# Four binary-convolution layers and attention on one core: the last image's softmax denominators by pixel halves in two PSUM tiles

## The chip, the cores and the metric

The kernel runs on one NeuronCore of a Trainium2 chip. A core has five engines with a queue of instructions each: TensorE (matmuls, PE in the profile; its weight loads are PEld), VectorE (DVE), ScalarE (ACT), GpSimd (POOL) and SyncE (SP), which issues DMAs. Every engine can also wait on semaphores and issue DMAs or branch; such instructions are run by its sequencer, and the profile marks them with a q (ACTq, SPq). The metric is the device time of one execution in microseconds (us). The median of three runs before the change is 949.11 us (948.44 to 949.25).

## The reference, cut to what matters

Input is x of shape 16 x 256 x 28 x 28. Three layers of binary convolutions come first (signs of activations, 3x3 convolutions, batch norms, gates); the change does not touch them. The fourth layer is attention within each image, over its N = 784 pixels:

```python
q = jnp.einsum('rc,bcn->bnr', Wq, xf)          # 64 channels
k = jnp.einsum('rc,bcn->brn', Wk, xf)
v = jnp.einsum('rc,bcn->bnr', Wv, xf)
attn = jnp.einsum('bnr,brm->bnm', q, k) * scale
attn = jax.nn.softmax(attn, axis=-1)
out = jnp.einsum('bnm,bmr->brn', attn, v)
out = jnp.einsum('cr,brn->bcn', Wp, out)
return out.reshape(B, C, H, W) + x
```

A softmax usually subtracts each row's maximum. The kernel's usual path leaves that out and keeps a watch: if a sum of exps (a denominator) or its reciprocal is too large, or an earlier stage has doubts about its arithmetic, a flag on the chip sends the program into a second, careful computation of the whole thing. With these inputs the flag says that all is well, and the careful program is jumped over.

## The kernel before, in words

`conv_seq_kernel` calls `forward(careful=False)`, which ends by loading the flag into a register of every engine (`values_load`, L1366), and then branches (`tc.If`, L80): in the usual case over the careful program, whose code lies between. After the branch, engines wait for the outstanding DMAs and drain.

Attention is `attend_unshifted` (from L1408). The order of instructions on every engine is written out by hand (`manual_schedule`): each engine runs its own instructions in the order of the code. An image has 7 chunks (`NC_`) of 112 keys. For chunk c of image b:

- `scores(b, c)`: two matmuls, one for each half (392) of the queries' pixels, into a tile of two PSUM banks (pool `pssc`, two buffers, "sc"), then one Exp on ScalarE over 128 x 784 into `es[b, c]` (L1502).
- `values(b, c)`: two matmuls side by side, each on 64 of the array's columns, that add the exps times v into one bank, `avs[b]` (pool `psav`). Rows 0 to 63 hold the first pixel half, rows 64 to 127 the second, so a tile of 128 x 392 (`HN`) holds an image.
- `denominators(b)`: the same with `ones` for v, into one bank "sm" (pool `pssm`, one buffer). For this, exps are added up first: `sum_up` adds chunks 0 to 3 on GpSimd (the sum called `sums[b, False]`, L1510 and L1512) and 4 to 6 on VectorE (`sums[b, True]`); `sum_all` (L1515) adds the two. That is for images up to 13. For images 14 and 15 (`b >= B - 2`, L1540) chunk 6 and the two sums stay apart, and TensorE adds them up, in three pairs of matmuls in place of one.
- `take_values(b)` copies `avs[b]` to SBUF (`o`) on ScalarE; `invert(b)` takes the reciprocals `r` on VectorE (L1545); `normalize(b)` multiplies o by r (L1549); `watch(b)` sums denominators and reciprocals on ScalarE with its accumulator into columns of `worst` (L1554).
- `project(b, mo)`: two matmuls with Wp for each half mo of the 256 output channels (L1579, pool `psmi`, one buffer "mi", or `pssc`); the function that it returns adds the residual on VectorE (L1590, or L1588 for banks apart). `store(b)` writes the image out (L1611).

Images overlap: while image b's scores are made, image b - 1 is normalized and b - 2 projected. After the loop, L1695 to L1720 hold what is left of images 13 and 14 beside image 15's scores; `doubts_so_far` (L1597) folds the earlier stages' doubts into `sure`. Then comes a block of its own (L1722), with a hint to each engine on where the branch will go. In it: the last values; reciprocals in two parts of 196 pixels of each half (`parts`); a copy of `avs` to SBUF (L1735); the watch on the denominators, in one accumulated sum, and on the reciprocals, half by ScalarE and half by VectorE (L1734 to L1737); the normalization in two parts; four projections of a part and a channel half each, and their additions. `raise_flag` (L1603) stands among these: VectorE adds up `worst` and compares it to LIMIT (L1605, L1606), a matmul counts the partitions that are well (L1607), and VectorE writes the flag (L1608). Channel half 0 is stored after its last addition, half 1 after the very last, both from ScalarE's queue.

Of the kernel before, what the change touches and what calls it, by code (L numbers as in the profile page):

```python
# [39 lines left out]
P = 128  # L40
B = 16
# [23 lines left out]

LIMIT = 1e18


VECS = (
    ["g0", "b0", "a_move", "a_alpha1", "a_alpha2"]  # L70
# [5 lines left out]


def conv_seq_kernel(tc: tile.TileContext, d: dict, out: bass.AP):
    again = forward(tc, d, out, False)
    with tc.If(again < 1, preferred_fallthrough_block=False, label="again") as usual:  # L80
        pass
    with usual.Else():
        forward(tc, d, out, True)


@with_exitstack
def forward(ctx: ExitStack, tc: tile.TileContext, d: dict, out: bass.AP, careful: bool):
# [1269 lines left out]
        return None  # L1357


    worst = const.tile([P, 4 * B], F32, name="worst")  # L1360
    nc.gpsimd.memset(worst, 0.0)
    flag = const.tile([P, 1], I32, name="flag")
    finish = (sg3, bg3, pt, x2d, x2, load_x2, idle)
    keys = [wpool.tile([P, NC_, 4, 32], F32, tag=t, name=f"keys{t}") for t in ("wa", "wa2")]
    attend_unshifted(tc, d, out, wqk, wv, wp, keys, worst, (doubts, nonzero), flag, pv, finish)
    return nc.values_load(flag[0:1, 0:1], min_val=0, max_val=P)  # L1366


@with_exitstack
# [39 lines left out]
def attend_unshifted(ctx, tc, d, out, wqk, wv, wp, keys, worst, doubts, flag, pv, finish):  # L1409
# [34 lines left out]
    def one_bank(pool, tag):  # L1444
        return pool.tile([P, 512], F32, tag=tag, name=tag)
# [71 lines left out]
    def side_by_side(ps, w, e, start, stop):  # L1517
        for h in range(2):
            T.matmul(ps[64 * h:64 * h + 64, :HN], lhsT=w, rhs=e[:, h, :], start=start, stop=stop)  # L1519
# [11 lines left out]
    def take_values(b, n=slice(0, HN)):  # L1531
        if n.start == 0:
            os[b] = (buf("o", 2, shape=(P, HN)), buf("r", 2, shape=(P, HN)))
        A.copy(os[b][0][:, n], avs[b][:, n])

    def denominators(b):

        dns[b] = last[:, 0, :HN] if b == B - 1 else one_bank(pssm, "sm")

        parts = [sums[b, False], sums[b, True], es[b, NC_ - 1]] if b >= B - 2 else [sums[b, True]]  # L1540
        for i, e in enumerate(parts):
            side_by_side(dns[b], ones.rearrange("p a i -> p (a i)"), e, i == 0, i == len(parts) - 1)

    def invert(b, n=slice(0, HN)):
        V.reciprocal(os[b][1][:, n], dns[b][:, n])  # L1545
# [46 lines left out]
        return add  # L1592


    w1, ok, sure, some = (ph.tile([P, 1], F32, name=n) for n in ("w1", "ok", "sure", "some"))

    def doubts_so_far():  # L1597
        V.tensor_reduce(sure, doubts[0], AX.X, ALU.max)
        V.tensor_scalar(sure, sure, 1.0, None, ALU.is_le)
        V.tensor_reduce(some, doubts[1], AX.X, ALU.min)  # L1600
        V.scalar_tensor_tensor(sure, some, K9 / 3.0, sure, ALU.is_ge, ALU.mult)

    def raise_flag(ps):  # L1603

        V.tensor_reduce(w1, worst, AX.X, ALU.add)  # L1605
        V.scalar_tensor_tensor(ok, w1, LIMIT, sure, ALU.is_le, ALU.mult)  # L1606
        T.matmul(ps[0:1, 0:1], lhsT=ok, rhs=turned[:, 0, 0:1], start=True, stop=True)  # L1607
        return lambda: V.tensor_scalar(flag[0:1, :], ps[0:1, 0:1], -1.0, float(P), ALU.mult, ALU.add)  # L1608

    def store(b, mo=slice(0, 2), queue=nc.sync):  # L1610
        queue.dma_start(out=out[b][:, mo], in_=x[b][:, mo])  # L1611
# [4 lines left out]
    with tc.manual_schedule(engines={ET.PE, ET.Activation, ET.DVE, ET.Pool, ET.SP}):  # L1616

        ps = [two_banks(psmi, "mi"), two_banks(pssc, "sc")]
        cuts = [slice(h * HN, h * HN + HN) for h in range(2)]
        for n in cuts:  # L1620
            v = x[0][:, 1, n]
            V.scalar_tensor_tensor(v, v, sg3[:, 1:2], x2[0][:, 1, n], ALU.mult, ALU.add)
        for h, n in enumerate(cuts):
            finish_a(0, n, (0,))
            v, w = (x[0][:, k, n] for k in range(2))
            A.activation(w, w, AF.Identity, bias=bg3[:, 1:2])
            V.tensor_tensor(v, v, x2[0][:, 0, n], ALU.add)
            for k, y in enumerate((v, w)):
                V.scalar_tensor_tensor(y, y, alpha[:, k:k + 1], y, ALU.mult, ALU.max)
            queries_keys(0, h, ps[h])  # L1630
        A.activation(ph.tile([P, 2], F32, name="e"), sg3, AF.Exp, scale=0.0)
        keep_busy(8)
        for h in range(2):
            keys_to(0, 1, h, ps[h])
            queries(0, h, ps[h])
            keys_to(0, 0, h, ps[h])
        finish_a(1)
        scores(0, 0)
        project_v(0)
        finish_b(1, ks=(0,))  # L1640
        turn_v(0)
        finish_b(1, ks=(1,))
        V.transpose(ones.rearrange("p a i -> p (a i)"), turned.rearrange("p a i -> p (a i)"))
        for b in range(B - 1):
            scores(b, 1)
            if b > 0:
                take_values(b - 1)
            if b == 0:
                finish_a(2)
            if b > 1:  # L1650
                project(b - 2, 0)()
            sum_up(b, 1)
            scores(b, 2)
            if b > 0:
                sum_up(b - 1, 6)
            scores(b, 3)
            sum_up(b, 2, 3)
            ps = two_banks(psmi, "mi")
            for h in range(2):
                queries_keys(b + 1, h, ps)  # L1660
            for h in range(2):
                keys_to(b + 1, 1, h, ps)
            for h in range(2):
                queries(b + 1, h, ps)
            for h in range(2):
                keys_to(b + 1, 0, h, ps)
            project_v(b + 1)
            if b > 0:
                sum_all(b - 1)
            turn_v(b + 1)  # L1670
            scores(b, 4)
            scores(b, 5)
            sum_up(b, 5)
            if b + 2 < B:
                finish_b(b + 2)
            if b + 3 < B:
                finish_a(b + 3)
            for c in range(4):
                values(b, c)
            if b > 0:  # L1680
                denominators(b - 1)
                invert(b - 1)
                normalize(b - 1)
            scores(b, 6)
            scores(b + 1, 0)
            if b > 1:
                project(b - 2, 1)()
                store(b - 2)
            if b > 0:
                watch(b - 1)  # L1690
            for c in range(4, NC_):
                values(b, c)


        b = B - 1  # L1695
        scores(b, 1)
        take_values(b - 1)
        project(b - 2, 0)()
        sum_up(b, 1)
        scores(b, 2)  # L1700
        denominators(b - 1)
        invert(b - 1)
        scores(b, 3)
        sum_up(b, 2, 3)
        normalize(b - 1)
        scores(b, 4)
        scores(b, 5)
        sum_up(b, 5)
        scores(b, 6)
        project(b - 2, 1)()  # L1710
        store(b - 2)
        doubts_so_far()
        for mo in range(2):
            project(b - 1, mo, pool=pssc)()
        store(b - 1)
        watch(b - 1)
        for c in range(3):
            values(b, c)
        last = two_banks(pssc, "sc")
        denominators(b)  # L1720

    with tc.block(), tc.manual_schedule(engines={ET.PE, ET.Activation, ET.DVE, ET.Pool, ET.SP}):  # L1722
        tc.mark_branch_hint_location("again", "LikelyTaken", engines=[ET.PE, ET.Activation, ET.DVE, ET.Pool, ET.SP])
        for c in range(3, NC_):
            values(b, c)

        parts = [slice(0, HN // 2), slice(HN // 2, HN)]
        os[b] = (buf("o", 2, shape=(P, HN)), buf("r", 2, shape=(P, HN)))
        r = os[b][1]
        watched = [worst[:, i:i + 1] for i in range(4 * b, 4 * b + 4)]  # L1730
        junk = buf("junk", 1, shape=(P, HN))
        for n in parts:
            invert(b, n)
        V.tensor_reduce(watched[2], r[:, parts[1]], AX.X, ALU.add)  # L1734
        A.copy(os[b][0], avs[b][:, :HN])  # L1735
        A.activation(junk, dns[b], AF.Copy, accum_out=watched[0])
        A.activation(junk[:, parts[0]], r[:, parts[0]], AF.Copy, accum_out=watched[1])  # L1737
        for n in parts:
            normalize(b, n)

        adds = [
            project(b, mo, ps, n) for n, mo, ps in (
                (parts[0], 0, two_banks(psmi, "mi")),
                (parts[0], 1, two_banks(pssc, "sc")),
                (parts[1], 0, [one_bank(pssm, "sm"), one_bank(psav, "av")]),
            )
        ]
        adds[0]()
        up = raise_flag(last[:, 1, :])
        adds.append(project(b, 1, two_banks(psmi, "mi"), parts[1]))  # L1750
        adds[2]()
        store(b, slice(0, 1), nc.scalar)
        up()
        for add in adds[1::2]:
            add()
        store(b, slice(1, 2), nc.scalar)


@with_exitstack
# [175 lines left out]
```

## Time and profile before

| what | value |
|---|---|
| median of three runs | 949.11 us (948.44 to 949.25) |
| the profiled execution's own time | 949.33 us |
| its span, first to last instruction | 947.5 us |
| granted TensorE clock, mean | 0.999 |
| TensorE, VectorE, ScalarE, GpSimd busy | 930.7, 757.1, 675.1, 139.0 us |
| image 14's denominators end, reciprocal, normalization | 924.16; 924.19 to 926.8; 926.90 to 928.34 us |
| image 15's denominators, last values | 932.20 to 934.17; to 936.83 us |
| last addition ends | 940.86 us |
| flag written | 939.9 us |
| last store issued; landed | 940.89; about 945.7 us |

Times within the execution are counted in us from the start of the span. A row of a timeline gives start, length, engine, line, operation, output <- inputs with their shapes (partitions x elements), and in brackets how long the engine had been idle before and what ended that. One row of TensorE can hold several matmuls ("x4"); a float32 matmul appears twice, so two matmuls side by side are an x4. Lines of the chain of waits give start, length and the instruction that the rest waited for. A line of an operation group gives minimum, median and maximum in nanoseconds, and the first and the last start.

### The profile page before, as it was taken

How to read it: one execution, taken by the hardware profiler on the slowest of the kernel's cores; microseconds unless marked ns; L12 is line 12 of the kernel's file. 1: busy time of each engine (PE TensorE's matmuls, PEld its weight loads, DVE VectorE, ACT ScalarE, POOL GpSimd, SP SyncE). 2: the span in 40 equal slices, each digit the busy share in tenths (PEclk: the TensorE clock that was granted, in tenths of full speed). 3: DMA queues.
4: the chain of work that ended last, by engine and by line, in shares of the span. 5: the costliest groups of instructions: out<-in, count | busy, mean ns of one | idle time of the engine just before them, and what ended most of it. 6: DMA issues, size and time to landing. Idle time of an engine off the chain costs nothing.

```text
span 947.5 us, 15043 instructions
## 1 busy us (share of the span) xinstructions
PE 930.7 (98%) x5636; PEld 583.2 (62%) x5636; DVE 757.1 (80%) x1446; ACT 675.1 (71%) x1179; POOL 139.0 (15%) x157
## 2 busy tenths in 40 slices
PE   7999999999999999999999999999999999999996
PEld 3555678788888878887555565556444444444442
DVE  3777798999998899987788878889656768687765
ACT  5665578888888888875777766775867666666652
POOL 2001100000000000000000000000334353534331
PEclk9999999999999999999999999999999999999999
DMA  9887434445533444421556211111132434434212
GB/s 346 287 303 264 168 121 138 165 181 198 198 139 139 148 156 164 160 86 50 223 209 214 113 40 59 79 78 59 35 68 70 112 92 94 112 78 126 69 68 106
DMA packets 39333, 130.70 MB, mean 138 GB/s; under 512 B 4866, under 2 KB 16324, under 8 KB 39252
## 3 DMA queue, kind: packets, MB, share of 16 engines
q1 hardware_dynamic: 33332, 98.31, 28.7%
q0 software_dynamic: 5632, 30.54, 11.7%
q8 instruction: 46, 0.75, 0.3%
q10 hardware_dynamic: 288, 0.80, 0.2%
q14 instruction: 35, 0.29, 0.1%
HBM read 72.67 MB, written 32.11 MB: 111 GB/s over the span
## 4 chain that ended last, share of the span: by engine, by line
PE 94%; DMA 1%; ACT 1%; DVE 1%; SPq 1%; issue 0%; DVEq 0%; ACTq 0%
PE cv L400 29%; PE cv L806 29%; PE sc L1498 8%; PE av L1519 8%; PE cv L933 5%; PE mi L1475 5%; PE sm L1561 2%; PE mi L1579 2%; PE unused L502 2%; PE sm L1519 1%; DMA xs<-in_x_dram 1%; PE gate L901 1%; PE hid L709 1%; DMA shifted<-fpads 1%; SPq L293 0%
## 5 line engine op out<-in xcount | busy, mean ns | idle before, releaser
L806 PE MATMUL cv<-vs,w 128*128 128x392 f32 (+1 forms) x1296 | 272.4, 352 | 0.3 <-DVE vs L137 0.3
L400 PE MATMUL cv<-fpads,wpk 128*128 128x392 f16 (+1 forms) x1458 | 247.8, 326 | 2.5 <-DVE wpk L325 1.2
L400 PEld LDWEIGHTS <-wpk 128*128 128x128 f16 x1782 | 171.5, 97 | 123.2 <-issue 3.1
L806 PEld LDWEIGHTS cv<-vs,w 128*128 128x128 f32 x768 | 143.2, 190 | 6.3
L1502 ACT ACTIVATE es<-sc 128x784 f32<-128x784 f32 x112 | 87.3, 822 | 41.4 <-PE sc L1498 41.4
L806 PEld LDWEIGHTS <-w 128*128 128x128 f16 x768 | 69.4, 99 | 51.9 <-issue 9.1
L1498 PE MATMUL sc<-q,keyswa 64*128 64x392 f32 x448 | 89.9, 513 | 0.9 <-ACT es L1502 0.9
L1519 PE MATMUL av<-es,v 128*64 128x392 f32 x448 | 80.7, 499 | 0.0
L1264 DVE SCALAR_TENSOR_TENSOR p<-ab,vec 128x392 f32<-128x392 int16 (+1 forms) x132 | 78.0, 605 | 0.0
L416 ACT ACTIVATE ab<-cv 128x392 int16<-128x392 f32 (+1 forms) x66 | 32.1, 486 | 56.3 <-PE cv L400 53.4
L1512 POOL TENSOR_TENSOR sum<-sum,es 128x784 f32<-128x784 f32 x32 | 67.2, 2099 | 3.1 <-ACT es L1502 0.6
L1498 PEld LDWEIGHTS sc<-q,keyswa 64*128 64x128 f32 x448 | 38.9, 186 | 44.0 <-issue 17.1
L400 PE MATMUL cv<-shifted,wpk 128*128 128x392 f16 (+1 forms) x324 | 60.6, 322 | 0.2 <-DMA shifted<-fpads 0.2
L806 PE MATMUL cv<-one_on,w 128*128 128x392 bf16 x240 | 59.4, 329 | 0.0
L961 POOL DMA_DIRECT2D x2d<-x x16 | 8.6, 536 | 345.3 <-DVE x L955 285.0
L1486 DVE COPY keyswa<-mi 64x392 f32<-64x392 f32 x31 | 16.3, 564 | 53.1 <-ACT q L1482 53.1
L1519 PEld LDWEIGHTS av<-es,v 128*64 128x64 f32 x448 | 29.4, 136 | 47.4 <-issue 47.0
L418 DVE SCALAR_TENSOR_TENSOR ab<-ab,cv 128x392 int16<-128x392 int16 (+1 forms) x66 | 36.0, 546 | 27.7 <-ACT ab L416 27.3
L788 ACT CAST vs<-vs 128x840 fp32r<-128x840 bf16 x63 | 54.1, 882 | 2.5 <-DVE vs L137 2.5
L933 PE MATMUL cv<-z,fw 128*128 128x392 f32 x256 | 48.9, 342 | 0.1
L933 PEld LDWEIGHTS cv<-z,fw 128*128 128x128 f32 x256 | 46.1, 188 | 0.9 <-ACT z L925 0.9
L1475 PE MATMUL mi<-p,wqk 128*128 128x392 f32 x124 | 45.1, 506 | 0.1
(323 smaller groups left out, 1531.2 us busy)
## 6 DMA issues: line engine op xcount, KB each, us to landing
xs<-in_x_dram SPq DMA_DIRECT2D x30, 784.0 KB, 5.1
one_on<-vs SPq DMA_DIRECT2D x60, 209.8 KB, 2.8
x2d<-x POOLq DMA_DIRECT2D x16, 784.0 KB, 3.6
out_dram<-p SPq DMA_DIRECT2D x15, 784.0 KB, 3.4
shifted<-fpads SPq DMA_DIRECT2D x26, 449.8 KB, 2.8
p<-x2d POOLq DMA_DIRECT2D x14, 784.0 KB, 6.7
p<-x2d SPq DMA_DIRECT2D x13, 784.0 KB, 5.7
n0d<-n POOLq DMA_DIRECT2D x16, 392.0 KB, 4.8
```

What stands on the lines that cost most here:

```text
L400: T.matmul(pss[j][:, n // size if careful else h, :rows * S].rearrange("p (a b) -> p a b", b=S), lhsT=w[:, n, c, :], rhs=src[:, blocks[j][ ...
L416: A.activation(by_halves(ab[:, 1], blocks[j]), ps, AF.Copy, scale=1.0 / PACK)
L418: V.scalar_tensor_tensor(a, b, -PACK, ps, ALU.mult, ALU.add)
L788: copy(v, w)
L806: T.matmul(ps.rearrange("p (a b) -> p a b", b=S), lhsT=w[:, k, c, u, mo * P:(mo + 1) * P], rhs=one_on[:, u, k, :, 0:S] if moved and c == 1 ...
L933: T.matmul(ps[:, h, :HN], lhsT=w[:, k, mo * P:(mo + 1) * P], rhs=z2[b][:, k, h * HN:(h + 1) * HN], start=(k + i == 0), stop=(k + i == 2),)
L1264: V.scalar_tensor_tensor(p, y, alpha[:, mo:mo + 1], y, ALU.mult, ALU.max, accum_out=mom.sums_at(at, mo)[0] if mom.by_sums(at, mo) else None,)
L1475: T.matmul(ps[:, h, :HN], lhsT=wqk[:, k, :], rhs=x[b][:, k, h * HN:(h + 1) * HN], start=(k == 0), stop=(k == 1))
L1498: T.matmul(ps[:, h, :HN], lhsT=chunk[rows], rhs=qs[b][rows], start=True, stop=True)
L1502: A.activation(e, ps[:, :, :HN], AF.Exp, scale=0.125)
L1512: (V if late else nc.gpsimd).tensor_tensor(sums[b, late], sums[b, late], e, ALU.add)
L1519: T.matmul(ps[64 * h:64 * h + 64, :HN], lhsT=w, rhs=e[:, h, :], start=start, stop=stop)
```

## The change

It touches only the end of attention, the watch, and how the flag and the branch are arranged.

- Image 14's and 15's exps are all summed on VectorE and GpSimd: `sum_up(b - 1, 6)` and `sum_all(b - 1)` stand after `take_values(b - 1)`, `sum_all(b)` stands where `doubts_so_far` stood. Image 14 then has one pair of denominator matmuls. Image 15 keeps chunk 6 apart, so it has two chunks of matmuls.
- `doubts_so_far` moves to a place before image 14's denominators. A fifth operation in it writes a further column of `worst`: 0 where all is well, 10 x LIMIT where not.
- Image 15's denominators are made by pixel parts of 196 in two PSUM tiles: part 0 in "sm", part 1 in the first bank of `last`.
- In the last block, VectorE takes the reciprocals part by part while ScalarE reads the denominators of the other part, twice: once to sum them, once through a Relu with a large negative scale, which is above zero only where a denominator is below 1e-5. The reciprocals are no longer watched for this image. The last values stand after that in the order; then the flag: ScalarE sums `worst`, a matmul adds the partitions up, VectorE compares the sum to LIMIT. The flag is now 1 in the usual case.
- `o` is made by multiplying `avs` in PSUM by r; ScalarE's copy is gone.
- Projections and additions run part 0 (both channel halves), then part 1. The flag is written before the first addition, and loaded into registers before the stores in the order of the code. There are three stores from ScalarE: part 0 of channel half 1, the whole of channel half 0, part 1 of channel half 1.
- The last block moves into a function `leave`, called within one block with the branch; pools are closed at its end.

```diff
+STEEP = 1e24
...
-    again = forward(tc, d, out, False)
-    with tc.If(again < 1, preferred_fallthrough_block=False, label="again") as usual:
-        pass
-    with usual.Else():
-        forward(tc, d, out, True)
+    leave = forward(tc, d, out, False)
+    with tc.block():
+        usually = leave()
+        with tc.If(usually > 0, preferred_fallthrough_block=False, label="again") as usual:
+            pass
+        with usual.Else():
+            forward(tc, d, out, True)
...
-    worst = const.tile([P, 4 * B], F32, name="worst")
+    worst = const.tile([P, 4 * B + 1], F32, name="worst")
...
-        dns[b] = last[:, 0, :HN] if b == B - 1 else one_bank(pssm, "sm")
-
-        parts = [sums[b, False], sums[b, True], es[b, NC_ - 1]] if b >= B - 2 else [sums[b, True]]
-        for i, e in enumerate(parts):
-            side_by_side(dns[b], ones.rearrange("p a i -> p (a i)"), e, i == 0, i == len(parts) - 1)
+        dns[b] = one_bank(pssm, "sm")
+        side_by_side(dns[b], ones.rearrange("p a i -> p (a i)"), sums[b, True], True, True)
+
+    def last_denominators(b, parts, banks):
+
+        dns[b] = [(n, t[:, 0:HN // 2]) for n, t in zip(parts, banks)]
+        for n, dn in dns[b]:
+            for i, e in enumerate((sums[b, True], es[b, NC_ - 1])):
+                for h in range(2):
+                    T.matmul(
+                        dn[64 * h:64 * h + 64], lhsT=ones.rearrange("p a i -> p (a i)"), rhs=e[:, h, n],
+                        start=(i == 0), stop=(i == 1),
+                    )
...
+    nc.gpsimd.memset(floor, STEEP * 1e-5)
...
         V.scalar_tensor_tensor(sure, some, K9 / 3.0, sure, ALU.is_ge, ALU.mult)
-
-    def raise_flag(ps):
-
-        V.tensor_reduce(w1, worst, AX.X, ALU.add)
-        V.scalar_tensor_tensor(ok, w1, LIMIT, sure, ALU.is_le, ALU.mult)
-        T.matmul(ps[0:1, 0:1], lhsT=ok, rhs=turned[:, 0, 0:1], start=True, stop=True)
-        return lambda: V.tensor_scalar(flag[0:1, :], ps[0:1, 0:1], -1.0, float(P), ALU.mult, ALU.add)
+        V.tensor_scalar(worst[:, 4 * B:], sure, -10.0 * LIMIT, 10.0 * LIMIT, ALU.mult, ALU.add)
+
+    def raise_flag(ps, junk):
+
+        A.activation(junk, worst, AF.Copy, accum_out=w1)
+        T.matmul(ps[0:1, 0:1], lhsT=w1, rhs=turned[:, 0, 0:1], start=True, stop=True)
+        return lambda: V.tensor_scalar(flag[0:1, :], ps[0:1, 0:1], LIMIT, None, ALU.is_le)
...
         take_values(b - 1)
+        sum_up(b - 1, 6)
+        sum_all(b - 1)
         project(b - 2, 0)()
         sum_up(b, 1)
         scores(b, 2)
+        doubts_so_far()
         denominators(b - 1)
         invert(b - 1)
...
         store(b - 2)
-        doubts_so_far()
+        sum_all(b)
...
         last = two_banks(pssc, "sc")
-        denominators(b)
...
+        last_denominators(b, parts, (one_bank(pssm, "sm"), last[:, 0, :]))
+
+    open_pools = ctx.pop_all()
+
+    def leave():
+        with tc.manual_schedule(engines={ET.PE, ET.Activation, ET.DVE, ET.Pool, ET.SP}):
+            tc.mark_branch_hint_location("again", "LikelyTaken", engines=[ET.PE, ET.Activation, ET.DVE, ET.Pool, ET.SP])
+            os[b] = (buf("o", 2, shape=(P, HN)), buf("r", 2, shape=(P, HN)))
+            o, r = os[b]
+            junk = buf("junk", 1, shape=(P, HN))
+            for i in (1, 0):
+                n, dn = dns[b][1 - i]
+                V.reciprocal(r[:, n], dn)
+                n, dn = dns[b][i]
+                at = 4 * b + 2 * i
+                A.activation(junk[:, n], dn, AF.Copy, accum_out=worst[:, at:at + 1])
+                A.activation(junk[:, n], dn, AF.Relu, bias=floor, scale=-STEEP, accum_out=worst[:, at + 1:at + 2])
+            for c in range(3, NC_):
+                values(b, c)
+            up = raise_flag(last[:, 1, :], junk[:, 0:4 * B + 1])
+            for n in parts:
+                V.tensor_tensor(o[:, n], avs[b][:, n], r[:, n], ALU.mult)
+            up()
+            adds = [project(b, mo, ps, parts[0]) for mo, ps in enumerate((two_banks(psmi, "mi"), two_banks(pssc, "sc")))]
+            for mo in range(2):
+                adds[mo]()
+                adds.append(project(b, mo, two_banks(pssc, "sc") if mo else two_banks(psmi, "mi"), parts[1]))
+            for mo in range(2, 4):
+                adds[mo]()
+            usually = nc.values_load(flag[0:1, 0:1], min_val=0, max_val=1)
+            by_parts = [halves(t[:, 1, :])[:, :, n] for n in parts for t in (out[b], x[b])]
+            nc.scalar.dma_start(out=by_parts[0], in_=by_parts[1])
+            store(b, slice(0, 1), nc.scalar)
+            nc.scalar.dma_start(out=by_parts[2], in_=by_parts[3])
+        open_pools.close()
+        return usually
```

More of the change, by code (lines that the diff above doesn't have):

```diff
@@ L1364, in forward @@
     keys = [wpool.tile([P, NC_, 4, 32], F32, tag=t, name=f"keys{t}") for t in ("wa", "wa2")]
-    attend_unshifted(tc, d, out, wqk, wv, wp, keys, worst, (doubts, nonzero), flag, pv, finish)
-    return nc.values_load(flag[0:1, 0:1], min_val=0, max_val=P)
+    finish_last = attend_unshifted(tc, d, out, wqk, wv, wp, keys, worst, (doubts, nonzero), flag, pv, finish)
+    open_pools = ctx.pop_all()
+    def leave():
+        usually = finish_last()
+        open_pools.close()
+        return usually
+    return leave
 @with_exitstack
@@ L1592, in project @@
         return add
-    w1, ok, sure, some = (ph.tile([P, 1], F32, name=n) for n in ("w1", "ok", "sure", "some"))
+    w1, sure, some, floor = (ph.tile([P, 1], F32, name=n) for n in ("w1", "sure", "some", "floor"))
+    nc.gpsimd.memset(floor, STEEP * 1e-5)
     def doubts_so_far():
@@ L1719, in attend_unshifted @@
         last = two_banks(pssc, "sc")
-        denominators(b)
[L1722 to L1725, printed above, removed]
-        parts = [slice(0, HN // 2), slice(HN // 2, HN)]
[L1728 to L1756, printed above, removed]
@@ new lines, in attend_unshifted, with leave @@
+        parts = [slice(0, HN // 2), slice(HN // 2, HN)]
+        last_denominators(b, parts, (one_bank(pssm, "sm"), last[:, 0, :]))
+    open_pools = ctx.pop_all()
+    def leave():
+        with tc.manual_schedule(engines={ET.PE, ET.Activation, ET.DVE, ET.Pool, ET.SP}):
[27 more added lines that the diff above has]
+            nc.scalar.dma_start(out=by_parts[2], in_=by_parts[3])
+        open_pools.close()
+        return usually
@@ L1759, in attend_shifted @@
+    return leave
 @with_exitstack
```

## The prediction

> **What bounds the kernel now.** The page first: TensorE is busy for 98% of the span, so a change of three microseconds in the last image can only matter where TensorE stands still or where nothing else is left to run. I therefore read the last 30 us three ways: the chain of waits in order of time, VectorE's and GpSimd's timelines, and the sequencer's lines after the branch.
>
> ```profile
> span 947.5 us, 15043 instructions
> PE 930.7 (98%) x5636; PEld 583.2 (62%) x5636; DVE 757.1 (80%) x1446; ACT 675.1 (71%) x1179; POOL 139.0 (15%) x157
> ```
>
> The chain (start, length, what) shows two places where VectorE, not TensorE, sets the pace: image 14's reciprocal and normalization (924.19 to 928.35), and everything from 936.83 on.
>
> ```profile
> 922.01 2.15 PE sm L1519 x12
> 924.19 2.62 DVE r L1545
> 926.90 1.45 DVE o L1549
> 928.48 1.59 PE sc L1579 x8
> 930.07 2.13 PE av L1519 x12
> 932.20 1.98 PE sc L1519 x12
> 934.17 2.66 PE av L1519 x16
> 936.85 0.49 ACT o L1735
> ```
>
> Twelve denominator matmuls take 1.98 to 2.15, so four (one chunk of exps, both halves) take 0.66. The timelines of VectorE and GpSimd show why the normalization takes 1.44 here and 0.57 an image earlier: it ends 0.43 after GpSimd's third sum (926.07 + 1.84 = 927.91).
>
> ```profile
> 918.22 0.57 DVE L1549 TENSOR_TENSOR o<-o,r 128x392 f32<-128x392 f32 x1
> 921.40 0.97 DVE L1590 TENSOR_TENSOR p<-mi,p 128x784 f32<-128x784 f32 x1 [1.73 <-PE mi L1579]
> 926.90 1.44 DVE L1549 TENSOR_TENSOR o<-o,r 128x392 f32<-128x392 f32 x1
> 923.58 1.84 POOL L1512 TENSOR_TENSOR sum<-sum,es 128x784 f32<-128x784 f32 x1
> 926.07 1.84 POOL L1512 TENSOR_TENSOR sum<-sum,es 128x784 f32<-128x784 f32 x1 [0.65 <-ACT es L1502]
> ```
>
> The last addition ends at 940.86; 6.6 us follow with no engine busy. The lines of the branch (first and last start at the end) and of the stores show what fills them.
>
> ```profile
> L80 SPq COMPARE_BRANCH  x1: 70/70/70, 940.8 to 940.8; - x1
> L80 SPq EVENT_SEMAPHORE  x8: 17/17/17, 944.7 to 945.7; - x8
> L1930 POOLq DRAIN  x3: 50/107/3897, 942.6 to 947.2; - x3
> DMA to landing us min/median/max: 2.5/3.3/4.8
> ```
>
> SP stands 3.8 us after its branch; VectorE (branch 940.9, next at 945.3) and ScalarE (941.9, 945.4) likewise 4.4 and 3.5. The last store is issued at 940.89 and lands 4.8 later, at 945.7, where SP's last waits on stores are; from there 1.8 us of waits and drains end the span. The first store took 2.5. Between them, seven packets on an instruction queue share the DMA engines.
>
> **What the Trainium skill says.** SBUF — State Buffer, "Who interferes with whom": a VectorE instruction with two SBUF inputs and a GpSimd instruction that reads SBUF lock each other out for the whole instruction. The trace agrees (1.44 against 0.57). ScalarE: Activation LUTs, "Table sets: the hidden batching unit": relu and copy are in every table set; the trace has four table loads of 1.28, the last at 668.87 for Exp, none around Copy, and one Relu group (L750) ran from 117.8 to 409.6 across the load at 140.70 without a load of its own. Runtime: NRT & Kernel Launch, "Instruction fetch mechanics": a taken branch outside the fetched window stalls for a fetch by DMA; the 3.5 to 4.4 after three branches agree.
>
> **The change, part by part** (times on the profiled execution's scale; 949.33 with its span of 947.5, so 1.8 lie outside the span; the median shown, 949.11, is 0.22 lower).
>
> 1. *Image 14's sums.* Added on VectorE: two 128x784 additions, 0.96 each. VectorE is idle from 919.67 and their inputs are ready (last exp 917.98, GpSimd's sum 911.6), so they run 919.7 to 921.5: free, hidden in the 1.73 of idle time, and just ahead of GpSimd's first sum at 921.64. If late, they would be locked out until 923.5. Removed on TensorE: two chunks of denominators, 2 x 0.66 = 1.32; these end at 922.65, not 924.16.
>
> 2. *The doubts moved ahead of image 14's reciprocal*, with one new VectorE operation: 0.28 + 0.15 + 0.16 + 0.16, by their rows, + 0.15. Before the reciprocal VectorE does the residual addition (to 922.4), then these; the fourth has two SBUF inputs and may wait for GpSimd's first sum (923.50). The reciprocal starts between 923.25 and 923.8, against 924.19, and ends by 926.4. Queued behind it: the normalization, for which TensorE waits.
>
> 3. *But the normalization still meets GpSimd.* Exp 3 now comes about 1.5 earlier (its scores stand behind the denominators on TensorE), so GpSimd's three sums run back to back: 921.64 + 3 x 1.86 + gaps and one turn for VectorE = 927.4. The normalization ends 0.43 later, 927.85 against 928.35: gain 0.5, not 1.3. TensorE idles about 1.5 at 926.5 instead. Bounds: +0.6 if the sums have no gap; -0.4 if VectorE's small operations lose their turn to GpSimd's second sum and the reciprocal starts only at 925.5.
>
> 4. *The last denominators.* In place of the doubts, VectorE adds image 15's two sums (0.96 against 0.75), done near 930.5, ahead of the denominators at 932.20 - 0.5 = 931.7. Behind it stand image 14's additions, which SP's store and the buffer of the second half's denominators wait for: from 930.4 to 932.25, not 930.69 to 932.54, and the first, 931.4, frees that buffer in time (needed 932.4). The new constant costs GpSimd one memset before image 0, under work of other engines. TensorE: two pixel halves x two chunks, 196 columns, by 0.33 (196-column groups at 938.22, 938.56 follow 0.34 apart) = 1.3 against 1.98: gain 0.66. The values then end at 936.83 - 0.5 - 0.66 = 935.7.
>
> 5. *Reciprocals and watching.* Two reciprocals of 1.31, from 932.4 (half one) to 935.1, stay under the values. ScalarE: four activations of 196 with their accumulator reads. By L1737's row 0.37 + 0.19, overlapping to 0.49, x 4 = 2.0; Relu's pointer bias adds 0.09 each by the skill's ScalarE page ("What ACT_TABLE_LOAD costs", an estimate). From 933.05 to 935.2, then the flag's activation, 0.45: 935.65. TensorE's flag matmul stands ahead of the projections; at 935.7 it is just ready. Cover gone, each further tenth on ScalarE delays all projections by a tenth.
>
> 6. *Normalizing from PSUM.* Removed: ScalarE's copy 0.49 with two handovers; VectorE's 0.36 reduction was under it. Before, the first normalization started 0.54 after the values (936.83 to 937.37); now 0.03: gain 0.5.
>
> 7. *Projections and additions.* Normalize 0.36, matmul 0.63, then four additions of 0.54. The third matmul reuses the one buffer that the first addition must empty: 937.3 + 0.7 = 938.05, then 0.56 + 0.45. The flag leaves the middle (w1 0.21, ok 0.16, flag 0.14 on VectorE). From the first normalization to the last addition: 3.36 against 3.49, gain 0.13. Last addition: 939.05 against 940.86, 1.8 earlier (0.5 + 0.66 + 0.5 + 0.13).
>
> 8. *Branch and stores.* The flag is set at 936.5, not 939.9; SP and GpSimd, which only wait for it, branch 3.4 earlier and stand through their fetch under the additions (SP to about 941.2). ScalarE's load of the flag (0.55) precedes the stores but ends at 937.1, before the first has data at 937.8: free. Three issues of 0.34 to 0.47 (strided rows by L780's, 0.47) instead of two: 937.8, 938.65, 939.1; the last carries 200 KB, not 392. Two, however, come close together, with VectorE's branch at 939.1 and ScalarE's at 939.6, so some fetches still collide with the last store. It lands 2.4 (no collision) to 4.8 (as before) after its issue; I take 4.0, since SP's fetch is out of the way. VectorE's stall to 943.4 sets a floor: a total gain of about 3.2. Tail gain 0 to 1.4; I take 0.7.
>
> Sum: 1.8 + 0.7 = 2.5: span 945.0, profiled time 946.8, median 949.11 - 2.5 = 946.6.
>
> **Rivals.** (B) The last store straggles as before, or the interleaved half-rows of the residual tile make the first two stores wait for the last addition too (issues 939.1, 939.55, 940.0). Gain 0.9 to 1.8: 947.3 to 948.2, say 947.8. For: landings spread from 2.5 to 4.8, and I can't place the fetches among them; against: 200 KB in place of 392. (C) VectorE loses its turn to GpSimd in step 2, so that image 14's normalization is 0.4 later than before and not 0.5 earlier: total gain 1.6, 947.5. For: GpSimd's gap between sums is 0.08; against: the addition that was locked out at 905.90 ended at 907.94, ahead of GpSimd's next sum, which was stretched to 2.46. (D) The other side: an instruction fetch of an engine in this last block. The branch hint and the branch lie around more code; if VectorE's, ScalarE's or TensorE's next page isn't there, it stands 3.5 to 4.4, as after the branches, before the last addition. With the tail as before that is -1.8 + 4.3: 951.6; it decides from a stall of 3.7. Against: the old block, similar in length, shows no such gap. (E) No change at all, if every gain is waited off at the stores: needs the landing 2.5 later than before; it lies inside B.
>
> **How the numbers follow.** Forecast 0.60 (its own range 945.7 to 947.2), B 0.22, C 0.10, D 0.08. About 0.2%, 1.9 us, is what a measurement of this kernel tells from no change. The forecast is below 947.2: faster 0.60. B, C and the milder quarter of D: same 0.34. The rest of D: slower 0.06. For 8 in 10, the range takes in the floor of step 8 (945.6 with scatter) and B's end: 945.6 to 948.4; what is left out is D and the ends.
>
> **What would show it.** Denominators of image 14: four matmuls, ended near 922.7; two VectorE additions of 0.96 before them, none near 2.0. The normalization of image 14 again longer than 1 us, ended about 0.4 after GpSimd's third sum. The last values ended near 935.7 with the first normalization within 0.1. No fifth table load. Flag matmul no later than 0.15 after the values. Last addition near 939.05; three stores, the last landing near 943. Wrong if the first two stores are issued after the last addition, if TensorE waits for the flag's activation, or if an engine stands over 3 us before 939.

## The result and the profile after

The changed kernel takes 947.35 us (median of 22 runs, 946.6 to 949.04) against 948.89 (22 runs, 948.44 to 950.08): a ratio of 0.9984, 95% interval 0.9978 to 0.9989. That is 1.54 us less, between 1.0 and 2.1. The gain is larger than the uncertainty of the measurement, but it is 0.16%, not clear of the 0.2% that the prediction had set as its bound. The forecast was 2.5 us.

The profiled execution took 948.88 and is one of the slower ones of its kernel. Its span:

```profile
span 947.1 us, 15041 instructions
```

Within its first 25 us it falls 1.5 us behind the profiled execution of before, long before any instruction that was edited. VectorE's last transposition but one, which is the same in both, starts at 896.47 before and at 897.78 after, 1.3 later. The profiled executions of nine variants below have this transposition between 896.0 and 896.7, so the 1.3 belongs to that one execution. I count from this transposition, called the mark below. From it to the end of the last addition it is 44.39 before (896.47 to 940.86) and 42.55 after (897.78 to 940.34): 1.84 earlier. From the last addition to the end of the span it is 6.6 before and 6.75 after.

The chain of waits of the changed kernel (start, length, what), which answers to the one shown in the prediction:

```profile
925.02 2.53 DVE r L1564
927.64 1.47 DVE o L1568
929.24 1.59 PE sc L1598 x8
930.83 2.12 PE av L1530 x12
932.95 0.66 PE sm L1558 x8
933.62 0.66 PE sc L1558 x8
934.28 2.66 PE av L1530 x16
936.96 0.37 DVE o L1765
```

Less 1.3, TensorE's projection of image 14 (L1598) starts at 927.9 and not at 928.5; image 15's denominators take 1.32 in place of 1.98; and the first normalization follows the last values at once (936.94 to 936.96), with no copy by ScalarE between.

What holds image 14 is in VectorE's and GpSimd's timelines of the changed kernel:

```profile
924.35 0.48 DVE L1621 SCALAR_TENSOR_TENSOR sure<-some,sure 128x1 f32<-128x1 f32 x1
927.64 1.46 DVE L1568 TENSOR_TENSOR o<-o,r 128x392 f32<-128x392 f32 x1
924.89 3.78 POOL L1523 TENSOR_TENSOR sum<-sum,es 128x784 f32<-128x784 f32 x2
```

The normalization again takes 1.46, and ends 0.43 after GpSimd's last sum (924.89 + 3.78 = 928.67). The one-element operation of the doubts with two SBUF inputs took 0.48 and not 0.16, while GpSimd's first sum (922.96 + 1.85) ended under it.

For the end, here are first the branch's instructions of the changed kernel, then the time from issue to landing of its second store and of its third:

```profile
L84 SPq COMPARE_BRANCH  x1: 70/70/70, 938.5 to 938.5; - x1
L84 SPq EVENT_SEMAPHORE  x8: 17/17/17, 941.1 to 945.4; - x8
L84 DVEq COMPARE_BRANCH  x1: 89/89/89, 940.7 to 940.7; - x1
L84 DVEq EVENT_SEMAPHORE  x1: 21/21/21, 945.1 to 945.1; - x1
```

```profile
DMA to landing us min/median/max: 4.9/4.9/4.9
DMA to landing us min/median/max: 5.0/5.0/5.0
```

SP branches early and runs on at 941.1, as was meant. It then waits for the last store, until 945.4. VectorE branches when its additions are done and stands 4.4, until 945.1. SP's waits after that show which of the two ended the span:

```profile
L1955 SPq EVENT_SEMAPHORE  x14: 17/28/28, 945.5 to 947.0; - x14
```

Twelve of them follow each other every 0.06 to 0.07 us and none takes longer than 28 ns, so SP found VectorE and ScalarE already there. The last landing (940.37 + 5.00 = 945.37) therefore decided the end; these waits, the drains and the engines' last waits for each other took the remaining 1.7. So the early flag moved SP's stall off the end, and the end stayed where it was.

### The profile page after: what moved, and what is told of

Read it like the earlier page. It is cut to its first block, busy times and chain, and to the rows that moved or that the text cites. A ratio compares the mean times of both kernels' runs of the same rounds, so it can differ in the third digit from the quotient of the medians.

```text
span 947.1 us, 15041 instructions
## 1 busy us (share of the span) xinstructions
PE 930.2 (98%) x5626; PEld 583.6 (62%) x5632; DVE 759.9 (80%) x1446; ACT 676.1 (71%) x1184; POOL 139.0 (15%) x158
## 4 chain that ended last, share of the span: by engine, by line
PE 95%; DVE 2%; ACT 1%; DMA 1%; issue 0%; SPq 0%; DVEq 0%; ACTq 0%
PE cv L404 31%; PE cv L810 29%; PE sc L1509 8%; PE av L1530 8%; PE cv L937 5%; PE mi L1486 5%; PE sm L1580 2%; PE unused L506 2%; PE mi L1598 2%; PE sm L1530 1%; PE gate L905 1%; DMA st<-in_w_dram 1%; PE hid L713 1%; DVE r L1564 1%; DVE p L1609 0%
```

## The experiments

All times in the table are from each kernel's own runs. "Addition" is the time from the mark to the end of the last addition, "tail" from there to the end of the span, both in one profiled execution of each kernel.

| kernel | median, us (runs) | ratio to before, interval | addition | tail |
|---|---|---|---|---|
| before | 948.89 (22) | | 44.39 | 6.6 |
| changed | 947.35 (22) | 0.9984, 0.9978 to 0.9989 | 42.55 | 6.75 |
| image 14's part alone | 948.43 (13) | 0.9995, 0.9986 to 1.0003 | 43.84 | 6.7 |
| last block alone | 947.77 (21) | 0.9989, 0.9982 to 0.9996 | 43.26 | 6.3 |
| changed, two stores | 947.54 (21) | 0.9985, 0.9978 to 0.9991 | 42.56 | 6.9 |
| changed, flag loaded after the stores | 947.19 (19) | 0.9982, 0.9975 to 0.9989 | 42.55 | 6.5 |
| changed, no branch | 944.33 (5) | 0.9951, 0.9938 to 0.9965 | 42.56 | 3.5 |
| changed, unread matmuls on TensorE | 946.89 (17) | 0.9976, 0.9969 to 0.9983 | 42.58 | 6.3 |
| changed, image 14 from PSUM | 946.29 (13) | 0.9974, 0.9966 to 0.9982 | 41.60 | 6.7 |
| the last two together | 946.03 (7) | 0.9971, 0.9960 to 0.9982 | 41.61 | 6.0 |
| changed, last image not stored | 945.62 (5) | 0.9963, 0.9949 to 0.9976 | 42.55 | 5.1 |

The kernel before had medians of 948.89 to 948.99 beside these.

### One part at a time

Image 14's part alone, on the kernel before:

```diff
-        ... if b >= B - 2 else [sums[b, True]]
+        ... if b == B - 1 else [sums[b, True]]
...
         take_values(b - 1)
+        sum_up(b - 1, 6)
+        sum_all(b - 1)
...
         scores(b, 2)
+        doubts_so_far()
         denominators(b - 1)
...
         store(b - 2)
-        doubts_so_far()
```

> The kernel before with image 14's part alone: its two sums added on VectorE, one pair of denominator matmuls, the doubts (four operations, as before) ahead of its reciprocal. Theory A (parts add up as the prediction sized them, GpSimd's sums hold the normalization back): the last addition 0.5 us earlier, the tail as before, 948.4 against 948.9. Theory B (TensorE's 1.3 us come through): 947.6. If image 14's part carries nothing: 948.9.

Measured: 948.43, the last addition 0.55 earlier. This is theory A, to a twentieth of a microsecond; TensorE was given back 1.3 us and used 0.55 of it. The interval reaches 1.0003, so the total alone does not show a gain; the trace shows the earlier addition.

The last block alone, on the changed kernel:

```diff
+        parts = [sums[b, False], sums[b, True], es[b, NC_ - 1]] if b == B - 2 else [sums[b, True]]
+        for i, e in enumerate(parts):
+            side_by_side(dns[b], ones.rearrange("p a i -> p (a i)"), e, i == 0, i == len(parts) - 1)
-        side_by_side(dns[b], ones.rearrange("p a i -> p (a i)"), sums[b, True], True, True)
...
-        sum_up(b - 1, 6)
-        sum_all(b - 1)
...
-        doubts_so_far()
         denominators(b - 1)
...
         store(b - 2)
+        doubts_so_far()
         sum_all(b)
```

> The changed kernel with image 14 as before (sums and chunk 6 apart on TensorE, doubts in their old place), so the new last block, the sum of image 15 and the new stores alone. Theory A: last addition 1.3 earlier than before, tail as in the changed kernel (0.15 longer), 947.8. Theory B: about 948.6, since most of the gain would be image 14's.

Measured: 947.77, the last addition 1.13 earlier. That the total is the 947.8 of theory A is partly luck: the addition gained 0.17 less than expected, and a tail longer than before by 0.15, which was expected too, did not come (in the profiled execution it is 0.3 shorter). Alone, the two parts give 0.55 + 1.13 = 1.68, together 1.84. Of the 0.16 between them, 0.15 is in image 15's denominators, which in this kernel take 0.68 + 0.79 in place of 0.66 + 0.66: the second half waits there for one of VectorE's residual additions (L1611), which frees the buffer.

### The normalization from PSUM

If GpSimd's third sum locks image 14's normalization out because the normalization reads two tiles in SBUF, then reading one of them, the values, from PSUM must free it. On the changed kernel:

```diff
-        take_values(b - 1)
+        os[b - 1] = (buf("o", 2, shape=(P, HN)), buf("r", 2, shape=(P, HN)))
         sum_up(b - 1, 6)
...
-        normalize(b - 1)
+        V.tensor_tensor(os[b - 1][0], avs[b - 1][:, :HN], os[b - 1][1], ALU.mult)
```

> The changed kernel with image 14 also normalized from PSUM (no copy of its values to SBUF), so that the multiplication has one SBUF input and not two. Theory A (GpSimd's third sum locks the normalization out): it takes about 0.55 and not 1.46, TensorE's projection of image 14 starts 0.9 earlier, the last addition too, 0.7 to 0.9 faster than the changed kernel, 946.5. Theory B (the 1.46 has another cause, or ScalarE's exps hold TensorE as long): within 0.3 of the changed kernel.

Measured: 946.29, 1.06 less than the changed kernel, and the last addition 0.95 earlier. From the timelines of GpSimd, VectorE and TensorE in this kernel:

```profile
923.60 3.78 POOL L1523 TENSOR_TENSOR sum<-sum,es 128x784 f32<-128x784 f32 x2
926.28 0.57 DVE L1728 TENSOR_TENSOR o<-av,r 128x392 f32<-128x392 f32 x1
926.77 1.45 DVE L1521 TENSOR_TENSOR sum<-es 128x784 f32<-128x784 f32 x1
926.17 0.82 PE L1598 MATMUL mi<-o,wp 64*128 64x392 f32 x4
927.00 1.59 PE L1598 MATMUL sc<-o,wp 64*128 64x392 f32 x8
```

The normalization takes 0.57, though GpSimd's third sum runs beside it until 927.38. It starts where it did (926.28; 927.64 less 1.3 is 926.3), so ScalarE's copy, which the edit also takes away, is not what was gained. The lockout has passed to the next operation with two SBUF inputs, an addition of exps (1.45 in place of 0.96), for which TensorE does not wait. TensorE's two projections follow each other with no idle time. The cause of step 3 is thereby shown. This kernel has a lower median than the two before it; its interval and the changed kernel's just overlap, and the trace shows where the gain comes from.

### What fills the tail

Two edits of the changed kernel were tried, each alone. The first has two stores, of 392 KB each, in place of three; the second puts the flag's load behind the stores.

```diff
-            nc.scalar.dma_start(out=by_parts[0], in_=by_parts[1])
-            store(b, slice(0, 1), nc.scalar)
-            nc.scalar.dma_start(out=by_parts[2], in_=by_parts[3])
+            for mo in range(2):
+                store(b, slice(mo, mo + 1), nc.scalar)
```

> The changed kernel with the two stores of before (channel half 0, then channel half 1 whole, 392 KB each) in place of three. If the strided 784-byte rows or the third store lengthen the tail (theory B): faster than the changed kernel by 0.3 to 1. If one DMA engine that is held up by an instruction block sets the landing (theory A): within 0.3 of the changed kernel, 947.3, and again one landing far behind the others.

```diff
-            usually = nc.values_load(flag[0:1, 0:1], min_val=0, max_val=1)
             ...
             nc.scalar.dma_start(out=by_parts[2], in_=by_parts[3])
+            usually = nc.values_load(flag[0:1, 0:1], min_val=0, max_val=1)
```

> The changed kernel with the flag loaded into the registers after the stores, as before. It only moves ScalarE's load and branch (by 0.6) behind the last store; SP and GpSimd load it as early as in the changed kernel. Theory A: the same to 0.4 slower, 947.3 to 947.7, by ScalarE's later fetch. If the early load is what spoils the tail: faster by 0.5 or more.

Measured: 947.54 and 947.19, both within 0.2 of the changed kernel and inside its interval. The second was expected to be the same or slower and came out 0.16 lower, which is not told from no change. Neither the number and shape of the stores nor the order of the load sets the tail.

The next kernel has no branch at all: the flag is computed and not looked at, its loads and the branch hints are gone, and the careful program isn't there.

```diff
-        usually = leave()
-        with tc.If(usually > 0, ...) as usual:
-            pass
-        with usual.Else():
-            forward(tc, d, out, True)
+        leave()
...
-            usually = nc.values_load(flag[0:1, 0:1], min_val=0, max_val=1)
```

> The changed kernel without the flag's load, the branch and the careful program behind it (the flag is computed and not looked at, so the second pass is left out). No engine has to fetch instructions from elsewhere at the end. Theory A (fetches hold up the last stores and the engines): the last store lands 2.3 to 2.6 after its issue in place of 5.0, the tail is some 4.3 to 4.8 in place of 6.75, and the time 945.0 to 945.5. Theory B (the strided rows are slow by themselves): landing 4 or more after the issue, time above 946.5.

Measured: 944.33, 3.0 less than the changed kernel and more than expected. The last addition is where it was (42.56); the whole difference is tail, 3.5 in place of 6.75. Below are the landings of the first and of the last store of this kernel, counted from their issue, and SP's waits:

```profile
DMA to landing us min/median/max: 2.1/2.1/2.1
DMA to landing us min/median/max: 2.6/2.6/2.6
L1947 SPq EVENT_SEMAPHORE  x11: 17/28/28, 932.6 to 942.5; - x11
```

The same strided rows land in 2.6 when no engine branches. The 3.2 of tail fall into two terms: the last landing comes 2.4 earlier after its issue (2.6 in place of 5.0), and the span ends 0.9 after it in place of 1.7, because SP has done most of its waits by then. The second term was in none of the estimates. In every kernel with branch and stores, the one before too, the span ends 1.7 to 1.8 after the last landing.

In the next kernel the last image is not stored (its output is left out), and flag and branch are kept:

```diff
-            nc.scalar.dma_start(out=by_parts[0], in_=by_parts[1])
-            store(b, slice(0, 1), nc.scalar)
-            nc.scalar.dma_start(out=by_parts[2], in_=by_parts[3])
```

> The changed kernel without the three stores of the last image (image 15's output is left out); the flag, its loads and the branch stay. If instruction fetches and stores hold each other up on the DMA engines (theory A): VectorE and ScalarE stand 2.5 to 3.5 us after their branches and not 4.3, SP has no landing to wait for, and the tail after the last addition is 4.3 to 5.3 in place of 6.75: 945.4 to 946.4. If the fetch alone takes 4.3 (theory B): VectorE resumes 4.3 after its branch as before, the tail is 5.8 to 6.2, 946.5 to 947.

Measured: 945.62, a tail of 5.1. The branch's lines on VectorE and ScalarE, and SP's last waits:

```profile
L84 DVEq COMPARE_BRANCH  x1: 89/89/89, 939.3 to 939.3; - x1
L84 DVEq EVENT_SEMAPHORE  x1: 21/21/21, 943.3 to 943.3; - x1
L84 ACTq COMPARE_BRANCH  x1: 68/68/68, 937.1 to 937.1; - x1
L84 ACTq EVENT_SEMAPHORE  x1: 17/17/17, 939.8 to 939.8; - x1
L1951 SPq EVENT_SEMAPHORE  x14: 17/28/1986, 940.8 to 944.3; - x14
```

The answer is mixed. The tail is as theory A has it, and ScalarE stands 2.7; but VectorE still stands 4.0, which is nearer to B, and SP waits 2.0 (the 1986 ns) for it. So with no store in sight, VectorE's stand after a branch that can't come before its last addition makes a tail of 5.1. It is not a fixed price: over the kernels with branch and stores VectorE stands 3.6 to 4.9. That it stands for a fetch is argued from the branch and from packets on the instruction queues; the last of these packets ended at 941.3, and what fills the 2.0 from there until VectorE ran on stays open. The stores' landing adds the other 0.9 to 1.8, though without a branch the stores need only 3.5 in all. Branch and stores together cost more than the longer of the two.

Why a store lands so late is in the records of single landings and packets. Of the second store of the changed kernel, fifteen DMA engines landed within 2.43 us of the issue and one at 4.85; of the third, twelve by 2.7, three by 3.4 and one at 5.0. Just before that last engine's packets, an instruction packet of 16 KB runs from 941.90 to 942.90; then follow, without a gap, eight packets of the second store and sixteen of the third, until 944.79. Each kernel with branch and stores shows such a packet 1.2 to 2.9 us after TensorE's branch. The queue that it is on moved 46 packets and 0.75 MB, and only TensorE, with over 11,000 instructions of matmul and weight load, has so many; the kernel without a branch shows none at its end. So I take it for TensorE's. To move it, 16 matmuls that nothing reads were put at TensorE's end:

```diff
+            for _ in range(16):
+                T.matmul(avs[b], lhsT=idle[:, 0:P], rhs=idle, start=True, stop=True)
             usually = nc.values_load(flag[0:1, 0:1], min_val=0, max_val=1)
```

> The changed kernel with 16 matmuls that nothing reads at the end of TensorE's queue, some 3.4 us, so that TensorE branches near 943.5 and not at 940.1, after the stores' data has moved. Theory A (TensorE's own 16 KB instruction block, fetched after its branch, holds up one DMA engine and with it the last two stores): all landings within 3.5 of the issue; then VectorE's and ScalarE's own fetches end last; 0.5 to 1.2 faster than the changed kernel, 946.2 to 946.9. If that block is not the cause: no change, or slower by TensorE's later end.

Measured: 946.89. The edit did less than was meant: the branch didn't wait for the matmuls. TensorE's unread matmuls (the trace has 15 of the 16) and its lines of the branch in this kernel:

```profile
938.15 3.40 PE L1774 MATMUL av<-idle 128*128 128x512 bf16 x15 [0.16 <-DVE p L1609]
L84 PEldq COMPARE_BRANCH  x1: 397/397/397, 938.7 to 938.7; - x1
L84 PEldq EVENT_SEMAPHORE  x1: 51/51/51, 941.6 to 941.6; - x1
```

It branched at 938.7, 0.1 after the last addition in place of 0.6 before it. The packet began 2.4 after the last addition in place of 1.6, so it was put off by 0.8 and not by 3.4. The second store then landed whole within 2.55; the third still took 4.5, three engines near 3.45. In the records the packet (940.99 to 942.03) now stands just ahead of the last rows of the third store (942.02 to 942.62). The gain of 0.46 is just below what A expected, and the intervals of the two ratios overlap: that the packet is in the way is supported, not settled.

The last kernel has both edits, image 14 from PSUM and the unread matmuls:

> Both edits together: image 14 normalized from PSUM, and 16 unread matmuls at TensorE's end. If both theories A hold the gains add up: 1.3 to 2.0 faster than the changed kernel, 945.4 to 946.0.

Measured: 946.03, 1.3 less than the changed kernel and 2.9 less than before, the lowest of the kernels that compute everything and keep the branch. The gains did not add up in full (1.06 + 0.46 = 1.5), and against image 14 from PSUM alone the 0.26 is not settled.

## Why the prediction was right, and where it was off

The direction was right and the time lay in the range, but the case that came is rival B (0.22; 947.3 to 948.2), not the forecast (0.60; 945.7 to 947.2). Of the chances, "within 0.2%" was given 0.34.

Steps 1 to 7 held in their mechanism, with small slips in size. Less the 1.3 of this execution: the denominators of image 14 end near 922.8 (step 1 wrote 922.65, but its own 924.16 - 1.32 is 922.84); the reciprocal starts at 923.6 (923.25 to 923.8), after an operation of the doubts that waited for GpSimd, as step 2 allowed; the normalization ends at 927.8 (927.85); the last values end at 935.6 (935.7); the last addition at 939.03 (939.05). By the experiments, image 14's part was 0.55 (0.5 forecast) and the block 1.13 alone, 1.29 beside image 14's part (1.3 forecast). That step 3's wait is GpSimd's lock is shown by the normalization from PSUM.

Step 5 missed a wait that cost nothing:

```profile
935.39 1.38 DVE L1756 RECIPROCAL r<-sc 128x196 f32<-128x196 f32 x1 [0.34 <-ACT junk L1760]
```

ScalarE's and VectorE's reads of one PSUM tile took turns here: the second reciprocal started at 935.39, when ScalarE's second read of that tile ended (935.36), and not when VectorE was free. It ended at 936.77 with the values at 936.94, so 0.17 of the cover was left, where step 5 had 0.6.

Step 8 failed, in a size and in its reason. The last store's landing, taken as 4.0 after its issue, took 5.0, so the tail gain of 0.7 came out at about -0.15; over the tails of the changed kernel and of the variants that keep its stores and branch order, 6.3 to 6.75, it is 0.3 at most. And its reason, that SP's fetch is out of the way, took SP's for the one that matters. The packet that stood before the stores came after TensorE's branch, and TensorE ran on 0.1 after that branch, so the view of stalls could not show it. Another view could: the prediction counted seven instruction packets after the last addition of before, all on one queue, and left out the eighth, of 16 KB on the other queue. The two rows (packets, MB, share of 16 engines) are from the stretch 940.9 to 948 of the kernel before:

```profile
q14 instruction: 7, 0.06, 2.9%
q8 instruction: 1, 0.02, 0.9%
```

In that kernel the packet ran from 942.56 to 943.56, while the last store was landing. The limit by VectorE's stall was named rightly: step 8 put the most that could be gained at 3.2, and without the stores the gain is 3.3.

Rivals C and D did not come: VectorE got its turn ahead of GpSimd's second sum, and no engine stood over 3 us for a fetch before the last addition. Relu needed no table load, and it took 0.42 against Copy's 0.33, the 0.09 that step 5 had estimated.

## What to carry to other kernels

When a stage is freed of work, look for what its consumer meets next: here 1.3 us taken off TensorE became 0.55, until the multiplication that waited for GpSimd was given an operand in PSUM. At the end of a kernel with a branch over much code, price the tail by the slowest of the sixteen landings of the last store, by the engine that branches last, and by the waits that come after both (5.0, 4.4 and 1.7 here). Moving SP's stall forward was worth nothing here while the last landing stayed late. An engine that shows no stall after its branch may still fetch, so count the packets on every instruction queue.

## What the runs showed of the hardware that I had not expected

The flag's loads and the jump over the careful program cost about 3.0 us of 947 together, all after the last addition (tail 6.75 with them, 3.5 without). TensorE's sequencer took the branch while matmuls before it were still queued: with 16 more of them it branched at 938.7, the matmuls ran until 941.55, and its next instruction behind the branch came at 941.6. And a VectorE operation on one element of each partition, with two SBUF inputs, waited a third of a microsecond for GpSimd (0.48 against 0.16).
